# Keys put in order by blocks of 16 heads in an attention kernel, with three of the eight blocks and the second chunk's adjacency squares moved inside the first chunk

## The chip, the cores and the metric

The kernel runs on one NeuronCore of a Trainium2 chip. The metric is the device time of one execution in microseconds (us). A core has five engines that run their own instruction queues in order: PE (TensorE, matmuls), DVE (VectorE), ACT (ScalarE), POOL (GpSimd) and SP (SyncE, which here only issues DMA transfers). They wait for each other and for transfers through semaphores. Sixteen DMA engines carry the transfers.

## The reference

Four graph layers over 3327 nodes with 128 features and an adjacency matrix `adj` (3327 x 3327). Nearly all of the time is the first layer, an attention whose "heads" come from a plain reshape of the projections:

```python
def _L0_gnn_ref(x, spatial_encoding, edge_encoding, Wq, Wk, Wv, Wo):   # both encodings are adj
    n, d = x.shape                       # 3327, 128
    h = Wq.shape[0] // d                 # 8
    scale = d ** (-0.5)
    q = (x @ Wq.T).reshape(d, n, h)      # 128 heads, each n keys of 8 elements
    k = (x @ Wk.T).reshape(d, n, h)
    v = (x @ Wv.T).reshape(d, n, h)
    a = jnp.einsum('dnh,dmh->dnm', q, k) * scale
    a = a + spatial_encoding + edge_encoding
    a = jax.nn.softmax(a, axis=2)
    out = jnp.einsum('dnm,dmh->dnh', a, v)
    return out.reshape(n, h * d) @ Wo.T
# x = x + layer 0..3 of relu(layernorm(x)); layers 1 to 3 are dense products with adj
```

So there are 128 heads of head size 8, and each one adds the same matrix 2 adj to its 3327 x 3327 scores.

## The kernel before

**Prelude.** The nodes are normalised and projected, 13 steps of two node tiles each. The keys go to DRAM as they come out (`kraw_d`, one row of 128 heads x 3327 keys for each of the 8 elements e), the queries to `qS_d`. Then the values are projected in 13 more steps, and in the last eight of these `k_halves(e)` puts the keys of element e in order: it loads all 128 heads of that element (one head to a partition, 3327 keys), and for each of two halves r of the key tiles ACT rounds them to the matmul's 32-bit format (`hi`), DVE subtracts (`lo`), and SP stores both to `kS_d`, [2 halves, 8 elements, 128 heads, 3328 keys]. The tile framework orders this part by itself. A kernel branch then follows (`tc.If(loose < 1)`); the attention is inside it.

**Attention.** The queries are cut into 7 chunks c of 476 columns. In a chunk there are 32 groups g of 4 heads; in a group 13 units q, each a pair of key tiles (the even and the odd one, r = 0 and 1). This part is ordered by hand (`manual_schedule`): one loop over slots, four to a unit, writes out every engine's queue. In a unit DVE first puts adj minus a bound on the row's maximum into a PSUM bank (`seed`), PE adds the scores of the four heads one after the other (`scores`: each head's product comes with the previous head's taken away), ACT takes the exponential after each (`exps`), and PE multiplies with the values into `po` (`values`). In units 0, 2, 5, 7 and 10 of each group (`BY_HAND`), DVE works one exponential itself as a polynomial (`hand_exp`), so that these units and those behind them are fuller on DVE than units 4, 9 and 12.

**What a group needs from DRAM.** In unit 1 of a group, `loads` issues for the next group 16 key transfers (`KT<-kS_d`, `load_k`), the first queries (`load_q`) and the values (`VR`). In units 3, 5 and 7 POOL writes negated queries (`negate_q`) and SP issues the next head's queries. In unit 8 POOL spreads the values (`spread_v`) and touches the last keys (`all_here`, tile `seen`). The next group's first score matmul waits for `seen`. All these transfers are issued on SP's one queue, in the order in which the loop writes them. In the program's order of waits SP's transfers take turns on eight semaphores, and one waits for the one eight before it to have landed, so that at most eight are under way.

**The squares.** A chunk's seeds need adj transposed (`adjT`) and a bound for each query row (`bound_d`). Both are made for the next chunk during the present one, by squares of 128 rows, 4 or 3 to a chunk (22 in all inside chunks 0 to 5: four in chunk 0 and 18 after it). `plan(u, f)` hangs a step on unit u; it is written out at the unit's start, after the first step of `hand_exp`. For each of a square's four quarters j, in one group each, the steps are: `load` (4 transfers of adj rows into the tile `rows`), two `turn`s (DVE transposes 13 tiles each into the tile `cols`), `largest` (DVE, row maxima). After the fourth quarter come `gather` (4 transfers with 4 bytes a row to `rowmax_d`), `back` (one transfer that reads them again, tile `four`), `finish` (two small DVE operations that wait for `four`, then the transfer `bound_d<-b`) and `store` (one transfer of `cols` to `adjT`, 3328 packets of 512 bytes). Both tiles exist once. Before the change, with u the start of the group after the fourth quarter:

```python
sq, u = Square(e_t, s), (c * NG + 7 * k + 1) * NQ
for j in range(4):
    plan(u, sq.load, j)
    plan(u + 4, sq.turn, j, 0)
    plan(u + 9, sq.turn, j, 1)
    plan(u + 12, sq.largest, j)
    u += NQ
for k, f in ((0, sq.gather), (1, sq.back), (7, sq.finish), (8, sq.store)):
    plan(u + k, f)
```

After the attention come the dense products of layers 1 to 3, which the change does not touch.

Of the kernel before, what the change touches and what calls it, by code (L numbers as in the profile page):

```python
# [10 lines left out]
F32 = mybir.dt.float32  # L11
# [3 lines left out]
F32R = mybir.dt.float32r  # L15
I32 = mybir.dt.int32
AF = mybir.ActivationFunctionType
ALU = mybir.AluOpType
# [4 lines left out]
P = 128  # L23
N = 3327
D = 128
H = 8
HD = D * H
NT = 26
NP = NT * P
NQ = NT // 2  # L30

KW = NP // 4
HEADS = D
GN = HEADS * N
GP = GN + 4 * P
NC = 7
CW = 476
AW = 19 * NT
NG = HEADS // 4
HALF_SCALE = 0.5 * D ** -0.5  # L40


# [46 lines left out]
def gnn_kernel(ctx: ExitStack, tc: tile.TileContext, x, adj, Wq, Wk, Wv, Wo, embed, layer,  # L89
               embed_bias, layer_bias, weight, bias, W_in, W_out, out):  # L90
    nc = tc.nc
# [11 lines left out]
    kraw_d = dram.tile([H, GP], F32, name="kraw_d")  # L103

    qS_d = dram.tile([2, H, GP], F32, name="qS_d")
    kS_d = dram.tile([2, H, HEADS, NP], F32, name="kS_d")
# [36 lines left out]
    class Small:  # L143


        def __init__(self, pool, pre):
            self.pool, self.pre, self.n = pool, pre, 0
# [116 lines left out]
    class Square:  # L264
# [8 lines left out]
        def load(self, j):  # L273
            if j == 0:
                self.cols = self.pool.tile([P, NT, P], F32, name="cols")
            self.rows = self.pool.tile([P, KW], F32, name="rows")
            n0 = self.s * P + 32 * j
            m = min(32, N - n0)
            if m < 32:
                nc.gpsimd.memset(self.rows, 0.0)  # L280
            for i in range(4):
                w = KW - (i == 3)
                nc.sync.dma_start(self.rows[32 * i:32 * i + m, :w], adj[n0:n0 + m, i * KW:i * KW + w])
            nc.gpsimd.memset(self.rows[96:P, KW - 1:KW], NOTHING)
# [27 lines left out]
    def square(pool, s, small):  # L312
        q = Square(pool, s, small)
        for j in range(4):
            q.load(j)
            q.turn(j, 0)
            q.turn(j, 1)
            q.largest(j)
        q.store()
        return q  # L320

    def head_rows(tensor):

        return bass.AP(tensor=tensor.tensor, offset=tensor.offset, ap=[[N, HEADS], [1, N]])

    with tc.tile_pool(name="a1", bufs=1) as a1, tc.tile_pool(name="a2", bufs=2) as a2, \
# [6 lines left out]
        h = a1.tile([P, NT, D], F32, name="h")  # L333
# [16 lines left out]
        for t0 in range(0, NT, 2):  # L350
            for s in "kq":
# [3 lines left out]
                for i in range(2):  # L355
                    t = t0 + i
                    sq = a4.tile([P, H, P], F32, name="sq")
                    for b in range(2):
                        ps = projected(s, t, b)
                        by_e = ps.rearrange("p (e i) -> p e i", e=4)  # L360
                        part = (slice(None), slice(4 * b, 4 * b + 4), slice(i * P, (i + 1) * P))
# [11 lines left out]
                for half in range(2) if s == "q" else ():  # L373
                    nc.sync.dma_start(places(qS_d, t0, 2, H, half * H * GP), st[half].bitcast(F32))
                nc.gpsimd.dma_start(bass.AP(tensor=n2_d[s].tensor, offset=n2_d[s].offset + t0 * P,
                                            ap=[[NT * P, P], [1, 2 * P]]), n2.rearrange("p t i -> p (t i)"))
# [32 lines left out]
            nc.vector.tensor_scalar(wide, fm1, BOUND_MAX, None, op0=ALU.is_gt)  # L409
            return wide  # L410

        def k_halves(e):
            raw = a2.tile([P, NP], F32, name="st_q0")
            nc.gpsimd.memset(raw[:, N:NP], 0.0)
            nc.sync.dma_start(raw[:, :N], head_rows(kraw_d[e]))
            of = raw.rearrange("d (p q r) -> d r q p", q=NQ, r=2)
            for r in range(2):
                hi = a2.tile([P, NQ, P], F32R, name="st_k0")
                lo = a2.tile([P, NQ, P], F32R, name="st_q1")
                nc.scalar.copy(hi, of[:, r])  # L420
                nc.vector.tensor_tensor(lo, of[:, r], hi.bitcast(F32), op=ALU.subtract)
                for i, half in enumerate((hi, lo)):
                    nc.sync.dma_start(kS_d[i, e, :, r * NQ * P:(r + 1) * NQ * P],
                                      half.bitcast(F32).rearrange("d q p -> d (q p)"))

        v_rows = v_d.rearrange("(p t) d -> p t d", t=NT)
        for t0 in range(0, NT, 2):
            if t0 == 0:
                wide = bound_scores()
            if t0 >= 10:  # L430
                k_halves(t0 // 2 - 5)
            sv = a2.tile([P, 2, HD], F32, name="st_v")
            for i in range(2):
                for b in range(2):
                    evac(sv[:, i, b * 512:(b + 1) * 512], projected("v", t0 + i, b))
            nc.gpsimd.dma_start(v_rows[:, t0:t0 + 2], sv)
# [3 lines left out]
    with tc.tile_pool(name="d1", bufs=1) as d1, tc.tile_pool(name="d2", bufs=2) as d2, \  # L440
# [17 lines left out]
        with tc.If(loose > 0):  # L458
            for s in range(squares_of(0), NT):
                square(d2, s, d2)  # L460
            for t in range(NT):
                m = rows_of(t)
                ar = d1.tile([P, NP], F32, name="ar")
# [61 lines left out]
    with tc.tile_pool(name="e1", bufs=1) as e1, tc.tile_pool(name="e_adj", bufs=28) as e_adj, \  # L525
# [73 lines left out]
        with tc.If(loose < 1), tc.manual_schedule():  # L599
# [80 lines left out]
            def bare(c, q):  # L680

                w = width_of(c)
                nc.scalar.activation(EA[q][:, :w], EA[q][:, :w], AF.Exp, scale=2.0)
# [71 lines left out]
            def plan(u, f, *a):  # L755
                behind.setdefault(u, []).append((f, a))

            def plan_squares(c):
                for k, s in enumerate(range(squares_of(c), squares_of(c + 1))):
                    sq, u = Square(e_t, s), (c * NG + 7 * k + 1) * NQ  # L760
                    for j in range(4):
                        plan(u, sq.load, j)
                        plan(u + 4, sq.turn, j, 0)
                        plan(u + 9, sq.turn, j, 1)
                        plan(u + 12, sq.largest, j)
                        u += NQ
                    for k, f in ((0, sq.gather), (1, sq.back), (7, sq.finish), (8, sq.store)):
                        plan(u + k, f)

            for j in range(4):  # L770
# [18 lines left out]
                        plan(u - (7 if c else 1), bare, c, q)  # L789
            shifted(0, 0)  # L790
            bare(0, 0)

            def in_slot(i):

# [715 lines left out]
```

## Time and profile before

| what | value |
| --- | --- |
| time, median of 3 runs | 10971.67 us (10970.61 to 10973.61) |
| profiled execution, its own time | 10981.99 us |
| its span, first to last instruction | 10980.2 us, so 1.8 us lie around it |
| PE busy | 10536.5 us (96%) |
| ACT busy | 10031.9 us (91%) |
| DVE busy | 8481.1 us (77%) |
| POOL busy | 1532.1 us (14%) |
| prelude: first instruction behind the branch | 419.65 us |
| first score matmul | 456.16 us |
| first and last copy of `po` (one to a group, 224) | 511.6 and 10172.7 us |
| a `turn`, a `largest` on DVE (median) | 991 and 1011 ns |
| granted TensorE clock, mean | 0.984 |

The 224 copies of `po` are 223 groups apart, so a group takes 43.3 us on average and a unit 3.33 us. In the timelines a line reads: start in us, length in us, engine, line of kernel.py, operation, out<-in by the program's tile names, count; in brackets the time that the engine sat idle before it, and what ended that. SPq is SP issuing transfers: its length is that of the issuing, not of the transfer. The line numbers are those of the kernel before.

### The profile page before, as it was taken

What the parts mean: (1) busy time and instruction counts of PE and PEld (TensorE: products, weight loads), DVE (VectorE), ACT (ScalarE), POOL (GpSimd) and SP (SyncE); (2) the same over time, 40 slices, a digit from 0 to 9 for tenths busy, and PEclk for the clock granted to TensorE, in tenths of its full rate; (3) what the DMA queues carried; (4) which work ended last, traced back from release to release, by engine and by line L of the source; (5) the groups of instructions that cost most, each with busy time, mean ns of one, the idle gap of its engine ahead of it and who ended that gap; (6) DMA issues with size and microseconds to landing.
All of it is one profiled execution on the core that took longest, in us unless ns stands there. A gap on an engine that the chain in (4) does not pass through costs nothing. (4 is left out here: it accounts for less than half of the span.)

```text
span 10980.2 us, 204468 instructions
## 1 busy us (share of the span) xinstructions
PE 10536.5 (96%) x72876; PEld 3438.3 (31%) x72876; DVE 8481.1 (77%) x13503; ACT 10031.9 (91%) x13789; POOL 1532.1 (14%) x2480
## 2 busy tenths in 40 slices
PE   4599999999999999999999999999999999999889
PEld 2133333333333333333333323333323333333544
DVE  5588887888878887788887888878877777777655
ACT  3599999999999999999999999999999999999330
POOL 5011111111111111111111111111111111111101
PEclk7799999999999999999999999999999999999999
DMA  8865665665565565565556555565555555554678
GB/s 249 254 99 94 96 96 111 96 97 95 89 119 94 96 97 86 109 99 93 90 95 118 94 96 93 94 118 97 87 92 96 97 94 87 81 88 72 203 235 281
DMA packets 695338, 1256.97 MB, mean 114 GB/s; under 512 B 195218, under 2 KB 555049, under 8 KB 691244
## 3 DMA queue, kind: packets, MB, share of 16 engines
q1 hardware_dynamic: 644044, 1114.42, 55.4%
q0 software_dynamic: 50272, 129.37, 4.3%
q8 instruction: 586, 9.60, 0.4%
q14 instruction: 436, 3.57, 0.1%
HBM read 1096.53 MB, written 146.60 MB: 113 GB/s over the span
## 5 line engine op out<-in xcount | busy, mean ns | idle before, releaser
L666 ACT ACTIVATE e<-S 128x952 f32<-128x952 f32 (+1 forms) x9024 | 8366.0, 1102 | 40.3 <-PE S L654 33.6
L713 PE MATMUL po<-e,VA 128*9 128x476 f32 (+1 forms) x46592 | 5739.3, 565 | 33.1 <-DVE OS L721 12.6
L645 DVE TENSOR_TENSOR S<-a,shb 128x476 f32<-128x476 f32 (+1 forms) x5824 | 3940.7, 677 | 1450.4 <-ACT e L666 1062.5
L654 PE MATMUL S<-QS,KT 64*128 64x476 f32 (+1 forms) x22176 | 4533.8, 445 | 77.8 <-DMA a<-adjT 23.3
L654 PEld LDWEIGHTS S<-QS,KT 64*128 64x128 f32 x22176 | 2077.0, 184 | 5103.7 <-ACT e L666 1281.6
L669 ACT ACTIVATE e<-S 128x476 f32<-128x476 f32 (+1 forms) x4128 | 2476.1, 714 | 24.1 <-PE S L654 23.6
L695 DVE SCALAR_TENSOR_TENSOR e<-e,h 128x476 f32<-128x476 f32 (+1 forms) x2240 | 1493.9, 667 | 77.0
L713 PEld LDWEIGHTS po<-e,VA 128*9 128x9 f32 x46592 | 691.0, 88 | 1606.3 <-issue 1487.9
L570 POOL TENSOR_SCALAR QS<-QS 128x476 fp32r<-128x476 f32 (+1 forms) x669 | 484.8, 725 | 4292.9 <-DMA QS<-qS_d 2457.6
L725 POOL DMA_DIRECT2D oT_d<-OS x896 | 471.9, 532 | 3665.3 <-DVE OS L721 3622.1
L691 DVE TENSOR_SCALAR h<-S 128x476 f32<-128x476 f32 (+1 forms) x1120 | 728.0, 650 | 327.0 <-PE S L654 322.5
L697 DVE SCALAR_TENSOR_TENSOR e<-e,EA 128x476 f32<-128x476 f32 (+1 forms) x1120 | 754.0, 673 | 0.0
L695 DVE SCALAR_TENSOR_TENSOR e<-h 128x476 f32<-128x476 f32 (+1 forms) x1120 | 743.6, 664 | 0.0
L1110 PE MATMUL pu<-strip,y 128*128 128x512 f32 (+2 forms) x1456 | 600.2, 566 | 30.3 <-DVE y L971 14.8
L654 PE MATMUL S<-QZ,KT 64*128 64x476 f32 (+1 forms) x1120 | 494.4, 441 | 10.6 <-DVE S L645 9.3
L1110 PEld LDWEIGHTS pu<-strip,y 128*128 128x128 f32 (+1 forms) x1456 | 271.4, 191 | 304.5 <-issue 271.1
L580 POOL COPY VA<-VR 128x832 f32<-128x832 f32 x224 | 245.6, 1097 | 24.7 <-DMA VR<-v_d 24.7
L1114 DVE TENSOR_REDUCE deg<-strip 128x1 f32<-128x1536 f32 (+1 forms) x104 | 193.7, 1881 | 62.1 <-DMA strip<-adjT 43.5
L654 PEld LDWEIGHTS S<-QZ,KT 64*128 64x128 f32 x1120 | 205.4, 183 | 87.1 <-DVE S L645 47.7
L288 DVE STREAM_TRANSPOSE cols<-rows 128x416 f32<-128x416 f32 x208 | 204.5, 988 | 30.6 <-DMA rows<-in_adj_dram 23.4
L721 DVE COPY OS<-po 128x476 f32<-128x476 f32 (+1 forms) x224 | 146.2, 653 | 88.8 <-PE po L713 88.8
L1063 ACT COPY uT<-pu 128x512 f32<-128x512 f32 (+1 forms) x21 | 11.1, 553 | 222.3 <-PE pu L1110 222.3
(256 smaller groups left out, 1956.7 us busy)
## 6 DMA issues: line engine op xcount, KB each, us to landing
KT<-kS_d SPq DMA_DIRECT2D x1792, 208.0 KB
KT<-kS_d SPq DMA_DIRECT2D x1792, 104.0 KB
VR<-v_d SPq DMA_DIRECT2D x224, 416.0 KB
QS<-qS_d SPq DMA_DIRECT2D x3072, 14.9 KB
QS<-qS_d SPq DMA_DIRECT2D x1536, 29.8 KB
adjT<-cols SPq DMA_DIRECT2D x26, 1664.0 KB
a<-adjT SPq DMA_DIRECT2D x156, 238.0 KB
strip<-adjT POOLq DMA_DIRECT2D x39, 895.5 KB, 5.5
```

The lines of the kernel that those rows point to most:

```text
L570: nc.gpsimd.tensor_scalar(QS[b][:, j + 1, :w], QS[b][:, j, :w].bitcast(F32), -1.0, 0.0, op0=ALU.mult, op1=ALU.add)
L580: nc.gpsimd.tensor_copy(VA[(c * NG + g) % 2][:, :, :, 0:H], v.rearrange("p j (t e) -> p t j e", e=H))
L645: touch(u, [r], nc.vector.tensor_tensor(bank(u, r), adj_of[c][2 * q + r][:, :w], shift_of[c][:, :w], op=ALU.subtract))
L654: x = nc.tensor.matmul(bank(u, r), KT[b][64 * r:64 * r + 64, max(0, j - 1), q * P:(q + 1) * P], q_s[64 * r:64 * r + 64, :w], start=hand an ...
L666: touch(u, (0, 1), nc.scalar.activation(e[:, :, :w], S[:, odd:even + 1, :w], AF.Exp, scale=2.0))
L669: touch(u, [r], nc.scalar.activation(e[:, 1 - r, :w], bank(u, r), AF.Exp, scale=2.0))
L691: touch(u, [1], nc.vector.tensor_scalar(s, bank(u, 1), EXP_ARG, None, op0=ALU.mult))
L695: nc.vector.scalar_tensor_tensor(e, s if k == 3 else e, EXP_C[k], s, op0=ALU.add, op1=ALU.mult)
L697: nc.vector.scalar_tensor_tensor(e, e, EXP_C[0], EA[pairs[u][2]][:, :w], op0=ALU.add, op1=ALU.mult)
L713: nc.tensor.matmul(po[32 * j:32 * j + H + 1, :w], VA[k % 2][:, 2 * pairs[v][2] + of, j, :], e_of[v, j][:, 1 - of, :w], start=(q == 0 and r ...
L725: nc.gpsimd.dma_start(oT_d[:, d * N + c * CW:d * N + c * CW + w], o[32 * j:32 * j + H + 1, :w])
L1110: nc.tensor.matmul(ps[:, :k], y[:m, t, :], s[:m, c * 4 * P - c0:c * 4 * P - c0 + k], start=(t == 0), stop=(t == NT - 1))
```

## The change

The keys are put in order by blocks b of 16 heads x 8 elements (128 partitions) instead of by element. Five blocks (`EARLY`) are done in the prelude, in its value steps 0, 2, 4, 6 and 8, as before on ACT and DVE (`k_block`). The other three (heads 80 to 127) are done inside chunk 0, planned from groups 16, 20 and 24 on (`Keys`): a load of 128 rows of 3327 keys into the tile `cols`, then four parts of 7 or 6 key tiles each; for each part DVE copies the rounded keys into the tile `rows` (`high`), SP stores them, POOL subtracts in place (`low`), SP stores again. The tile `rows` grows from 832 to 896 columns.

The squares of chunk 0 start at groups 0, 4, 8 and 12 instead of 1, 8, 15 and 22, one unit later within the group (unit 1), each next one right behind the last. Their `gather` and `store` come right before the next start. In all chunks `back` moves from 1 to 9 and `finish` from 7 to 12 units behind the group's start; in chunks 1 to 5 `gather` stays at 0 and `store` at 8.

In the order of the changed program's SP queue, chunks 1 to 5 have: `rowmax_d<-rm` x4, the 16 keys, values and queries of the next group, `adjT<-cols`, `four<-rowmax_d`, `bound_d<-b`, the next 16 keys. Before it was `rowmax_d<-rm` x4, `four<-rowmax_d`, the 16 keys, values and queries up to the third head's, `bound_d<-b`, the fourth head's queries, `adjT<-cols`, the next 16 keys.

```diff
--- before.py
+++ after.py
@@ -37,6 +37,8 @@
 CW = 476
 AW = 19 * NT
 NG = HEADS // 4
+KB = P // H
+EARLY = 5
 HALF_SCALE = 0.5 * D ** -0.5
 
 
@@ -273,7 +275,7 @@
         def load(self, j):
             if j == 0:
                 self.cols = self.pool.tile([P, NT, P], F32, name="cols")
-            self.rows = self.pool.tile([P, KW], F32, name="rows")
+            self.rows = self.pool.tile([P, 7 * P], F32, name="rows")[:, :KW]
             n0 = self.s * P + 32 * j
             m = min(32, N - n0)
             if m < 32:
@@ -318,6 +320,29 @@
             q.largest(j)
         q.store()
         return q
+
+    def k_rows(b):
+
+        return bass.AP(tensor=kraw_d.tensor, offset=kraw_d.offset + KB * b * N, ap=[[N, KB], [GP, H], [1, N]])
+
+    def k_store(b, i, r, q0, half):
+        m = half.shape[-1]
+        nc.sync.dma_start(bass.AP(
+            tensor=kS_d.tensor, offset=kS_d.offset + (i * H * HEADS + KB * b) * NP + (r * NQ + q0) * P,
+            ap=[[NP, KB], [HEADS * NP, H], [1, m]]), half)
+
+    def k_block(b, pool):
+        raw = pool.tile([P, NP], F32, name="st_q0")
+        nc.gpsimd.memset(raw[:, N:NP], 0.0)
+        nc.sync.dma_start(raw[:, :N], k_rows(b))
+        of = raw.rearrange("d (p q r) -> d r q p", q=NQ, r=2)
+        for r in range(2):
+            hi = pool.tile([P, NQ, P], F32R, name="st_k0")
+            lo = pool.tile([P, NQ, P], F32R, name="st_q1")
+            nc.scalar.copy(hi, of[:, r])
+            nc.vector.tensor_tensor(lo, of[:, r], hi.bitcast(F32), op=ALU.subtract)
+            for i, half in enumerate((hi, lo)):
+                k_store(b, i, r, 0, half.bitcast(F32).rearrange("d q p -> d (q p)"))
 
     def head_rows(tensor):
 
@@ -409,26 +434,12 @@
             nc.vector.tensor_scalar(wide, fm1, BOUND_MAX, None, op0=ALU.is_gt)
             return wide
 
-        def k_halves(e):
-            raw = a2.tile([P, NP], F32, name="st_q0")
-            nc.gpsimd.memset(raw[:, N:NP], 0.0)
-            nc.sync.dma_start(raw[:, :N], head_rows(kraw_d[e]))
-            of = raw.rearrange("d (p q r) -> d r q p", q=NQ, r=2)
-            for r in range(2):
-                hi = a2.tile([P, NQ, P], F32R, name="st_k0")
-                lo = a2.tile([P, NQ, P], F32R, name="st_q1")
-                nc.scalar.copy(hi, of[:, r])
-                nc.vector.tensor_tensor(lo, of[:, r], hi.bitcast(F32), op=ALU.subtract)
-                for i, half in enumerate((hi, lo)):
-                    nc.sync.dma_start(kS_d[i, e, :, r * NQ * P:(r + 1) * NQ * P],
-                                      half.bitcast(F32).rearrange("d q p -> d (q p)"))
-
         v_rows = v_d.rearrange("(p t) d -> p t d", t=NT)
         for t0 in range(0, NT, 2):
             if t0 == 0:
                 wide = bound_scores()
-            if t0 >= 10:
-                k_halves(t0 // 2 - 5)
+            if t0 % 4 == 0 and t0 // 4 < EARLY:
+                k_block(t0 // 4, a2)
             sv = a2.tile([P, 2, HD], F32, name="st_v")
             for i in range(2):
                 for b in range(2):
@@ -458,6 +469,8 @@
         with tc.If(loose > 0):
             for s in range(squares_of(0), NT):
                 square(d2, s, d2)
+            for b in range(EARLY, HEADS // KB):
+                k_block(b, d1)
             for t in range(NT):
                 m = rows_of(t)
                 ar = d1.tile([P, NP], F32, name="ar")
@@ -755,16 +768,46 @@
             def plan(u, f, *a):
                 behind.setdefault(u, []).append((f, a))
 
+            class Keys:
+
+                def __init__(self, b):
+                    self.b = b
+
+                def load(self):
+                    raw = e_t.tile([P, NT, P], F32, name="cols").rearrange("p t n -> p (t n)")
+                    nc.gpsimd.memset(raw[:, N:NP], 0.0)
+                    nc.sync.dma_start(raw[:, :N], k_rows(self.b))
+                    self.of = raw.rearrange("d (p q r) -> d r q p", q=NQ, r=2)
+
+                def high(self, r, q0, q1):
+                    self.part = e_t.tile([P, 7 * P], F32, name="rows")[:, :(q1 - q0) * P]
+                    nc.vector.tensor_copy(self.part.rearrange("d (q p) -> d q p", p=P).bitcast(F32R),
+                                          self.of[:, r, q0:q1, :])
+                    k_store(self.b, 0, r, q0, self.part)
+
+                def low(self, r, q0, q1):
+                    part = self.part.rearrange("d (q p) -> d q p", p=P)
+                    nc.gpsimd.tensor_tensor(part.bitcast(F32R), self.of[:, r, q0:q1, :], part, op=ALU.subtract)
+                    k_store(self.b, 1, r, q0, self.part)
+
+            def plan_keys():
+                for b in range(EARLY, HEADS // KB):
+                    u, keys = 4 * (b - 1) * NQ + 1, Keys(b)
+                    plan(u, keys.load)
+                    for hi, lo, r, h in ((7, 9, 0, 0), (13, 16, 0, 1), (22, 24, 1, 0), (26, 30, 1, 1)):
+                        plan(u + hi, keys.high, r, 7 * h, 7 + 6 * h)
+                        plan(u + lo, keys.low, r, 7 * h, 7 + 6 * h)
+
             def plan_squares(c):
                 for k, s in enumerate(range(squares_of(c), squares_of(c + 1))):
-                    sq, u = Square(e_t, s), (c * NG + 7 * k + 1) * NQ
+                    sq, u = Square(e_t, s), (c * NG + 7 * k + 1 if c else 4 * k) * NQ + (not c)
                     for j in range(4):
                         plan(u, sq.load, j)
                         plan(u + 4, sq.turn, j, 0)
                         plan(u + 9, sq.turn, j, 1)
                         plan(u + 12, sq.largest, j)
                         u += NQ
-                    for k, f in ((0, sq.gather), (1, sq.back), (7, sq.finish), (8, sq.store)):
+                    for k, f in ((0 if c else -1, sq.gather), (8 if c else -1, sq.store), (9, sq.back), (12, sq.finish)):
                         plan(u + k, f)
 
             for j in range(4):
@@ -789,6 +832,8 @@
                         plan(u - (7 if c else 1), bare, c, q)
             shifted(0, 0)
             bare(0, 0)
+
+            plan_keys()
 
             def in_slot(i):
 
```

## The prediction, made before the changed kernel ran

> **What bounds the kernel now.** I read the page's busy shares, a table by windows, the prelude's timeline, then SP's queue and DVE around one square, and last the longest stall of DVE inside the attention.
>
> ```profile
> PE 10536.5 (96%) x72876; PEld 3438.3 (31%) x72876; DVE 8481.1 (77%) x13503; ACT 10031.9 (91%) x13789; POOL 1532.1 (14%) x2480
> ```
>
> ```profile
> 350.00:400.00 50.00, 0.00 (x0) 0.00 (x0) 19.58 (x8) 22.73 (x9) 0.83 (x4) 0.51 0.92 368
> ...
> 600.00:700.00 100.00, 99.13 (x728) 30.07 (x728) 82.95 (x129) 99.93 (x139) 12.35 (x22) 1.00 0.58 87
> ```
>
> Columns after the window and its length: busy us and instructions of PE, weight loads, DVE, ACT, POOL; clock; DMA share; GB/s. The prelude's end (first row) is DMA alone: share 0.92, PE idle. In the attention PE and ACT are full, and 728 matmuls in 100 us is the pace with and without a square under way. So time is won only in the prelude, and in the attention lost only where PE is made to wait; nothing lost there is caught up.
>
> The prelude, the last pairs of elements:
>
> ```profile
> 358.36 1.37 SPq L415 DMA_DIRECT2D st_q<-kraw_d  x2
> 366.39 6.58 ACT L420 CAST st_k<-st_q 128x1664 fp32r<-128x1664 f32 x2 [11.81 <-DMA st_q<-kraw_d]
> ...
> 376.39 0.33 SPq L423 DMA_DIRECT2D kS_d<-st_q  x1
> ...
> 413.88 0.33 SPq L423 DMA_DIRECT2D kS_d<-st_q  x1
> 419.65 1.69 POOL L601 MEMSET VA<- 128x936 f32 x2 [34.11 <-SPq L458]
> ```
>
> SP's queue at the end of chunk 1's first square:
>
> ```profile
> 2059.24 1.75 SPq L299 DMA_DIRECT2D rowmax_d<-rm  x4
> 2066.97 0.38 SPq L304 DMA_DIRECT2D four<-rowmax_d  x1
> 2067.44 12.98 SPq L551 DMA_DIRECT2D KT<-kS_d  x16
> ...
> 2101.65 0.53 SPq L295 DMA_DIRECT2D adjT<-cols  x1
> 2105.18 12.61 SPq L551 DMA_DIRECT2D KT<-kS_d  x14
> ```
>
> The 4-byte writes of `gather` take about 6 us to land, `back` waits for that, and the keys start 6.3 us late (one group earlier they started at 2018.0, so 2061.1 was due). The store comes a whole group later. Its packets, two DMA views:
>
> ```profile
> DMA packets 3539, 2.16 MB, mean 196 GB/s; under 512 B 113, under 2 KB 3485, under 8 KB 3538
> ```
>
> ```profile
> DMA packets 150, 0.65 MB, mean 161 GB/s; under 512 B 53, under 2 KB 53, under 8 KB 150
> ```
>
> The first is 2101 to 2112, the second 2112 to 2116: the store's 3328 packets of 512 B are all in the first, so it takes up to 10.4 us. The store of 5183.91, which had no small write just before it, had all of them through by 5191.2: with the landing about 8 us. DVE at unit 12 of the same group:
>
> ```profile
> 2101.26 0.64 DVE L697 SCALAR_TENSOR_TENSOR e<-e,EA 128x476 f32<-128x476 f32 x1
> 2102.87 0.66 DVE L645 TENSOR_TENSOR S<-a,shb 128x476 f32<-128x476 f32 x1 [0.96 <-ACT e L666]
> ```
>
> The last rows show what a late DVE costs (here for a late `rows` in chunk 5), on DVE and on PE:
>
> ```profile
> 8187.75 0.65 DVE L697 SCALAR_TENSOR_TENSOR e<-e,EA 128x476 f32<-128x476 f32 x1
> 8197.31 0.96 DVE L288 STREAM_TRANSPOSE cols<-rows 128x416 f32<-128x416 f32 x1 [8.92 <-DMA rows<-in_adj_dram]
> ```
>
> ```profile
> 8191.77 0.69 PE L654 MATMUL S<-QS,KT 64*128 64x476 f32 x3
> 8200.33 0.76 PE L654 MATMUL S<-QZ,KT 64*128 64x476 f32 x1 [7.87 <-DVE S L645]
> ```
>
> A DVE wait of 8.9 us in a free unit cost PE 7.9: about 1 us is free.
>
> **1. Prelude.** In the changed program's order the first four blocks stand where the first four elements stood, with the same loads, casts and stores; then one block comes in place of four elements. It is the first of the pair loaded at 358.36: its fourth store is the one of 376.39. From the last store to the first instruction behind the branch it was 419.65 - 413.88 = 5.8 us, so that instruction comes at 382.2: **-37**. Bounds -30 (the four stores, now 16 x 8 rows in eight places, each take 2 us more) and -42 (no second load in the same queue).
>
> **2. `back` leaves the keys' way (18 squares, chunks 1 to 5).** Mostly hidden before: `seen` lay 9 us ahead of the first scores in a group without squares (1701.5 against 1712.2). Groups with it lost little, one 6 us (copies of `po` at 5145.2 and 5194.5, 49.3 apart instead of 43.1). Together **-10** (0 to -13).
>
> **3. `finish` behind the store (the same 18).** The change lets `store` pass ahead of `back` in SP's queue, and `finish` waits for `four` at unit 12 of that very group, on DVE, with the next seeds behind it. From the free time of the key buffer, t = 2061.1: an undisturbed group has its last queries issued 34.7 us after the first keys (1711.34 to 1746.0). The first four key pieces now go at t, the rest when the 4-byte writes have landed at about t+5, 2 us late: last queries t+37, store t+37.3, landed t+45.6 (8.3 us), `four` right behind it in the same queue, t+46.2. DVE reaches `finish` when the polynomial ends, 2101.9 = t+40.8. It waits 5.4 us; the two small operations add 0.4, and 0.96 was idle: 4.9 for PE, say 5. 18 x 5 = **+90**. Bounds: 3 each with the queries at t+35 (+54); 8.5 with them at t+38.5 and a 10.4 us store (+153).
>
> The Trainium skill (page "DMA: Bandwidth & Descriptors", section "Specifications") gives about 358 GB/s as a core's HBM limit; by that the store's 1.70 MB would land in an estimated 4.8 us, each wait would shrink to about 1.5 us and this term to about 27 us. The 8.3 to 10.4 us of the trace decide. The same page ("Queues, rings and completion order") says that descriptors are taken in ring order and a completion signal lands only after earlier writes of its DMA engine; that speaks against putting a waited-for read behind a long store.
>
> **4. Chunk 0, more steps on the same queues.** No row shows these together; bounds by the nearest.
> - Three square-to-square joints: `gather`, `store` and the next four loads now go ahead of the keys. The 16 keys take 20.5 us to land once started; they start when the store has landed, some 12 us late, against the 9 us of cover of `seen`. 3 each, **+10** (0 to 20).
> - `finish` of these squares at the next unit 0: `back` is issued after the late queries: 3 us of DVE wait each, three times, **+9** (0 to 15).
> - The joint to block 5: its load goes into `cols`, so SP waits for the store to land and then the load takes 4 to 8 us; keys 17 late less 9, +8; and that square's `four` stands behind the first `high` and `low` stores, +9: **+17** (5 to 30).
> - The three blocks: the second and fourth `high` are planned in unit 1, the store of the `low` before in SP's queue behind the fourth head's queries, 7 us before the next keys. `high` store 3 us (a store of twice the size took 3.4), POOL 1.8 us by its 512-column sum (996 ns), 3.5 if strides double it, `low` store 3 us: DVE waits 1 to 3 us for `rows` twice a block, and the keys behind it start 7 late, inside the cover. Each `high` is 896 x 2.0 ns = 1.8 us (by the prelude's strided subtraction, 3333 ns for 1664), or 0.6 by a contiguous pass (1954 ns for 3328); 0.8 stand out in full units. 2 x 2.5 + 1 + 4 x 0.8 = 9, three times **+27** (6 to 45).
> - Turns and `largest`, one unit later, fall in units 5, 10 and 0, which are DVE's own. There DVE idles 0.4 to 0.6 us before a seed and the step takes 1.0: 0.3 x 48 = **+14** (0 to 24).
>
> The sum is +77 (30 to 130). The three blocks' 15 MB find DMA at a share of 0.58 here, and POOL is 14% busy: both are cover; without it the keys would be late in every group. The wider `rows` and the untaken branch cost nothing.
>
> **Sum.** -37 - 10 + 90 + 77 = +120 on the profiled execution's 10981.99, so 11102. The median of the runs lies 10.3 us lower: 11092.
>
> **Rivals.** (A) *Faster: the read of `rowmax_d` passes the store.* If `four` lands within 3.5 us of its issue, unit 12 waits for nothing and term 3 is zero; with chunk 0 at 20, -37 - 10 + 20 = -27: 10945. For it: sixteen DMA engines and a tiny read. Against: the keys of 2105.18 do not show their packets until the store's are done. (B) *The store takes 10.4 us each time*, because the queue is as busy as at 2101: term 3 is 18 x 8 = 144, 11146. (C) *The prelude's gain does not come*: eight places for each store and load make one block as slow as two elements, the branch is left at about 413 and the gain is 6: 11123.
>
> **Chances.** Forecast 0.53, A 0.15, B 0.14, C 0.10, and 0.08 that the gain and a small term 3 cancel. A measurement of this kernel can tell about 0.2% (22 us) from no change; A lies 27 below, and one case in seven of it falls inside that bound: faster 0.13, same 0.10, slower 0.77. The range, 10950 to 11205, begins just above A, takes in the low ends of terms 3 and 4 (-42 - 13 + 54 + 30 = +29, so 11001) and the cancelling case, and goes up to their high ends not quite all together; half of A and the extreme of B are left out.
>
> **What would show it.** Right: the first instruction behind the branch near 382; in chunks 1 to 5, 18 DVE waits of 4 to 8 us before the reduction of `four`, put down to its transfer, and PE gaps of the same size; those groups 48 us apart by the copies of `po`, all others 43.1; chunk 0 some 75 us above 32 x 43.1. Wrong: no DVE wait at `four` (A), waits near 10 (B), the branch left at 410 or later (C), or chunk 0 as smooth as before.

## The result, and the profile after

The changed kernel takes 11095.5 us (median; 11090.1 to 11113.6) against 10971.1 us before, a ratio of 1.0116 (95% interval 1.0098 to 1.0133): about 124 us slower. The forecast was 11092. That it came so close is partly luck: one step of the sum failed by 27 us and another was too large by some 40, in opposite directions. Besides, the forecast went from a profiled execution that lay 10 us above its median, and the one profiled here lies 5 us below its own: between the two profiles the time grows by 108 us, where the sum has +120.

The page's busy shares after:

```profile
PE 10586.5 (95%) x72876; PEld 3444.5 (31%) x72876; DVE 8484.0 (77%) x13509; ACT 10024.4 (90%) x13783; POOL 1561.8 (14%) x2492
```

The instructions of PE are the same in number; the span has grown by 108 us, 10980.2 to 11088.3, and PE is busy for 50 us more of it. The table by windows, with the columns of before:

```profile
350.00:400.00 50.00, 9.44 (x17) 3.33 (x15) 14.36 (x10) 13.04 (x9) 1.60 (x3) 0.67 0.80 250
600.00:700.00 100.00, 94.64 (x680) 28.65 (x672) 78.54 (x123) 93.83 (x128) 12.05 (x20) 0.97 0.65 102
```

The first row is the prelude's end: DMA moves 250 GB/s here where it moved 368, and PE still has V work (17 matmuls) that had been done by 350 us before. The second row is in chunk 0: 680 matmuls instead of 728, so PE waits.

The end of the prelude in the timeline, the last block from its load to the first instruction behind the branch:

```profile
373.42 2.59 SPq L337 DMA_DIRECT2D st_q<-kraw_d  x1
...
392.60 6.58 ACT L342 CAST st_k<-st_q 128x1664 fp32r<-128x1664 f32 x2 [19.29 <-DMA st_q<-kraw_d]
402.54 0.54 SPq L330 DMA_DIRECT2D kS_d<-st_q  x1
410.66 1.69 POOL L614 MEMSET VA<- 128x936 f32 x2 [35.62 <-SPq L469]
```

One load takes 19 us where a load at the same place took 8 (358.36 to 366.4). Not all of that is the load's own doing: in the trace's packet records the stores of V (8192 bytes a packet) go on until about 389 here and were through by 359 before, and this load's packets took 0.55 us (median) against 0.50 for an element's. The branch is left at 410.7, only 9 us earlier than at 419.65.

One square of chunk 1, its second: SP's queue, then DVE and PE around unit 12.

```profile
2468.92 0.56 SPq L297 DMA_DIRECT2D adjT<-cols  x1
2469.53 4.12 SPq L306 DMA_DIRECT2D four<-rowmax_d  x1
2478.53 0.36 SPq L312 DMA_DIRECT2D bound_d<-b  x1
```

```profile
2472.77 0.65 DVE L710 SCALAR_TENSOR_TENSOR e<-e,EA 128x476 f32<-128x476 f32 x1
2478.15 0.16 DVE L310 TENSOR_REDUCE b<-four 128x1 f32<-128x4 f32 x1 [4.73 <-DMA four<-rowmax_d]
```

```profile
2477.06 0.69 PE L667 MATMUL S<-QS,KT 64*128 64x476 f32 x3
2480.59 0.75 PE L667 MATMUL S<-QZ,KT 64*128 64x476 f32 x1 [2.84 <-DVE S L658]
```

The read of `four` is issued right behind the store and comes back 8.6 us later; DVE stands for 4.7 us; the seed behind it is late, and PE stands for 2.8. The whole group is 4.6 us longer than 43.1, because the matmuls behind the wait are slow as well: the granted clock (third number from the end) is at half just then.

```profile
2480.60:2484.00 3.40, 3.40 (x13) 0.89 (x13) 3.19 (x5) 1.15 (x2) 0.00 (x0) 0.51 0.60 24
```

All squares together, from the view of the tile `four` (idle us of DVE, times):

```profile
  DMA four<-rowmax_d: 75.7, 21
```

Before, this line did not exist.

Chunk 0, where the last square hands over to block 5: SP's queue and PE.

```profile
1177.11 0.56 SPq L779 DMA_DIRECT2D cols<-kraw_d  x1
1177.78 20.56 SPq L564 DMA_DIRECT2D KT<-kS_d  x16
...
1216.62 1.53 PE L667 MATMUL S<-QS,KT 64*128 64x476 f32 x4 [9.47 <-POOL seen L597]
```

SP waits for the adj store to land (1177.1), loads the block, and the keys behind it need 20.6 us to be issued (12.3 to 13 in groups without a square). PE stands for 9.5 us, and another 6.7 at 1229.1 behind this square's late `four`. The group is 66.7 us long by the copies of `po`.

By those copies the span's 108 us divide so: prelude to the first copy -10.4; chunk 0 +78.1 (1420.2 us for 31 groups, 1342.1 before); chunks 1 to 5 +39.5; chunk 6 and all behind it +0.9. Chunk 0 by itself, from its first copy to its last, before and after:

```profile
511.55:1853.65 1342.10, 1329.69 (x9674) 407.58 (x9676) 1088.14 (x1673) 1338.71 (x1823) 180.53 (x294) 1.00 0.60 99
501.20:1921.40 1420.20, 1355.95 (x9674) 410.54 (x9676) 1112.87 (x1683) 1346.57 (x1823) 209.72 (x308) 0.98 0.62 104
```

The same 9674 matmuls keep PE busy 26.3 us longer, at a mean clock of 0.98 instead of 1.00; the other 51.8 of the 78.1 us are idle time of PE. In chunks 1 to 5 the 39.5 us are 24.3 of idle time and 15.2 of slower matmuls. In the attention of the changed kernel the granted clock falls to half 19 times, for 3.4 to 10.2 us (3 times before), and each time this begins during a gap of PE of 1.3 us or more, or within 2 us after one. So a wait of PE costs more than its own length here.

### The profile page after: what moved, and what is told of

The parts are those of the page before. It is cut to its first block, busy times and chain, and to the rows that moved or that the text cites. A ratio compares the mean times of both kernels' runs of the same rounds, so it can differ in the third digit from the quotient of the medians.

```text
span 11088.3 us, 204505 instructions
## 1 busy us (share of the span) xinstructions
PE 10586.5 (95%) x72876; PEld 3444.5 (31%) x72876; DVE 8484.0 (77%) x13509; ACT 10024.4 (90%) x13783; POOL 1561.8 (14%) x2492
## 5 line engine op out<-in xcount | busy, mean ns | idle before, releaser
L658 DVE TENSOR_TENSOR S<-a,shb 128x476 f32<-128x476 f32 (+1 forms) x5824 | 3945.6, 677 | 1432.5 <-ACT e L679 1040.3
```

Source lines behind the costliest of these rows:

```text
L658: touch(u, [r], nc.vector.tensor_tensor(bank(u, r), adj_of[c][2 * q + r][:, :w], shift_of[c][:, :w], op=ALU.subtract))
```

## Experiments

Landing times below are issues and completions as the trace has them. "Square groups" are groups 5, 12, 19 and 26 of chunks 1 to 5: their sum above 43.1 us each was 13.7 before and is 54.4 after. Each time stands beside the runs of the kernel before on the same chip, whose median was 10969 to 10981.

**The finish alone.** `e1_finish_later`:

```diff
-  ... (9, sq.back), (12, sq.finish)):
+  ... (9, sq.back), (17 if c else 12, sq.finish)):
```

> The changed kernel with one number changed: in chunks 1 to 5 the step that reduces the four bounds (finish) runs five units later, at unit 17 instead of 12, that is in unit 4 of the next group. Theory (finish waits on DVE for a read that stands behind the adj store in SP's queue, and PE pays): the 18 DVE waits of 2 to 5 us before the reduction go, the groups 5, 12, 19 and 26 of chunks 1 to 5, 54 us above 43.1 in the changed kernel, fall to within 5 us in sum, and the time falls by about 50, from 11095 to some 11045. Rival (the groups are long because the late store and its read hold up the next keys, not DVE): the DVE waits go but the groups stay long, time within 15 us of 11095.

Measured 11052.9 us, 43 below the changed kernel (1.0066 of before, 1.0049 to 1.0083). The line for the tile `four` now reads:

```profile
  DMA four<-rowmax_d: 12.2, 4
```

These four are chunk 0's. The square groups stand 3.4 us above 43.1 in sum. So the wait on DVE is the whole of it: 54.4 - 3.4 = 51 us in the profile. Chunks 1 to 5 together are 47 us shorter than in the changed kernel: 30 us less idle time of PE, and 18 less for the same 49922 matmuls (6871.95 us busy instead of 6889.56).

**The same move in the kernel before.** `e2_before_late_back`:

```diff
-  ((0, sq.gather), (1, sq.back), (7, sq.finish), (8, sq.store)):
+  ((0, sq.gather), (8, sq.store), (9, sq.back), (12, sq.finish)):
```

> The kernel before with the offsets of the changed one alone: store at unit 8, back at unit 9, finish at unit 12, for all squares of the attention; prelude and placing of the squares as before. Theory (this move costs about 54 in waits and gives about 14 back, independent of the rest): some 40 us slower than before in chunks 1 to 5 and some 5 to 15 more for the four squares in chunk 0, so 11010 to 11030. Rival (the waits come from the squares being crowded or shifted by the new chunk 0): within 15 us of 10971.

Measured 11059.3 us, +81 (1.0074; 1.0057 to 1.0091), more than expected. DVE waited for `four` 22 times, 89.7 us in all; square groups 68.9, chunk 0 14 us longer. The cost belongs to the order of these steps, not to the new chunk 0.

**The good order by itself.** `e6_before_good_order`, the kernel before:

```diff
+  ((0, sq.gather), (8, sq.store), (9, sq.back), (17, sq.finish)):
```

> The kernel before with the squares' steps in a third order: store at unit 8, back at unit 9, finish at unit 17 (unit 4 of the next group). Theory (the changed kernel's early store and late back are good by themselves and only its finish is too early): the late keys of before go without a new wait, the groups 5, 12, 19 and 26 of chunks 1 to 5 stand within 5 us of 43.1 in sum (13.7 before, 68.9 with finish at unit 12), time 5 to 15 us below the kernel before. Rival (the queue pays somewhere else for the store ahead of the read): same as before or slower.

Measured 10978.8 against 10980.4 (0.9997; 0.9987 to 1.0007): no difference that can be told; the 5 to 15 us that were expected are not seen. The profile does show the late keys gone (square groups 3.3 instead of 13.7), so the 10 us of step 2 exist in this view, but the times can't confirm them.

**Eight blocks in the elements' places.** `e4_blocks_in_place`, the kernel before with the changed kernel's `k_block`:

```diff
-                k_halves(t0 // 2 - 5)
+                k_block(t0 // 2 - 5, a2)
```

> The kernel before with only the shape of the eight key steps in the prelude changed: eight blocks of 16 heads x 8 elements at the places where the eight elements of 128 heads stood, all in the prelude, nothing moved to the attention. The bytes and the number of transfers are the same. Theory (a block is slower than an element by its addresses): with 150 us for five blocks against 154 for eight elements, a block costs up to 1.5 times an element, and the prelude becomes 30 to 80 us longer, time 11000 to 11050; chunks 0 to 6 as before within 5 us. Rival (blocks cost what elements cost, and the gain was lost because the V work of the prelude is late): within 10 us of 10971.

Measured 11013.2, +35 (1.0032; 1.0020 to 1.0045). The branch is left at 456.5, 36.8 later than with elements, and nothing else moved (chunk 0 at 1341.4). The same bytes in the same number of transfers cost 4.6 us more for each block. The mark in the timeline is how soon ACT gets the buffer of a first store back. First the kernel before, then this one:

```profile
369.73 0.34 SPq L423 DMA_DIRECT2D kS_d<-st_k  x1
373.21 3.39 ACT L420 CAST st_k<-st_q 128x1664 fp32r<-128x1664 f32 x1 [0.24 <-DMA kS_d<-st_k]
```

```profile
430.87 0.58 SPq L329 DMA_DIRECT2D kS_d<-st_k  x1
436.33 3.34 ACT L341 CAST st_k<-st_q 128x1664 fp32r<-128x1664 f32 x1 [2.19 <-DMA kS_d<-st_k]
```

3.5 us against 5.5. SP too needs 0.58 us instead of 0.34 to issue it. The changed kernel has five such blocks: taking three out gives 456.5 - 410.7 = 46 us, and the shape had taken 37 of them beforehand.

**Why a block is slow.** Four kernels ask whether it is the addresses. `e3_element_major`, the changed kernel:

```diff
-  ap=[[N, KB], [GP, H], [1, N]])
+  ap=[[GP, H], [N, KB], [1, N]])
   ...
-  ap=[[NP, KB], [HEADS * NP, H], [1, m]]), half)
+  ap=[[HEADS * NP, H], [NP, KB], [1, m]]), half)
```

> The changed kernel with the 128 rows of a block taken in another order: partition = element x 16 + head instead of head x 8 + element, in load and store alike; the same bytes and packets. Theory (a block's transfers are slow because neighbouring partitions lie in eight far places): a store alone lands in 3.4 to 4 us instead of 5.4, a load alone in 8 to 10, the prelude's end comes 20 to 30 us earlier (first instructions behind the branch at 382 to 392 instead of 411), time 11065 to 11075. Rival (eight far places cost as much in any order, or something else than the transfers is late): prelude's end within 5 us of 411, time within 10 us of 11095.

Measured 11201.0 (1.0206; 1.0189 to 1.0223); branch left at 465.4, a lone store (one with little else under way) 8.5 to 10 us. Both expectations failed: it is much worse. The trace shows nine completions for each of these transfers where the others have sixteen. For the store issued at 442.72 the first of the nine comes 1.1 us after the issue and the other eight 6.8 to 8.5 us after it (of the sixteen of an element's store none comes before 3.2 us): with a first dimension of 8, eight engines carry it. So this run does not tell about addresses. The Trainium skill (page "DMA: Bandwidth & Descriptors", section "Rules for kernel authors") says that an outermost dimension of size c below 16 confines a transfer to at most c engines; the eight late completions fit that.

`e5_spread_heads`, as e4:

```diff
-  kraw_d.offset + KB * b * N, ap=[[N, KB], [GP, H], [1, N]])
+  kraw_d.offset + b * N, ap=[[H * N, KB], [GP, H], [1, N]])
```

and the store alike.

> Eight blocks in the prelude at the elements' places, as in e4, but each block takes every eighth head (b, b + 8, ...) instead of 16 neighbours. The number, size and bytes of the transfers stay; the sixteen first-dimension steps of a transfer now lie 104 KB apart, as they do for an element, instead of 13 KB. Theory (near addresses taken at the same time are what makes a block slow): a store alone lands in 3.4 to 4 us instead of 5.4, the first instruction behind the branch comes near 420 instead of 456.5, time within 12 us of the kernel before (10978). Rival (the far steps from element to element within one row group are what is slow): stores stay at 5.4, the branch is left between 450 and 460, time 11005 to 11020.

Measured 11019.5 (1.0035; 1.0023 to 1.0047), branch left at 462.0, a lone store 5.4 us. Near addresses are not the cause.

`e9_rows_together`, the changed kernel:

```diff
-  kS_d = dram.tile([2, H, HEADS, NP], F32, name="kS_d")
+  kS_d = dram.tile([HEADS, 2, H, NP], F32, name="kS_d")
   ...
-  ap=[[NP, KB], [HEADS * NP, H], [1, m]]), half)
+  ap=[[2 * H * NP, KB], [NP, H], [1, m]]), half)
```

> The changed kernel with another layout of kS_d: head, half, element, position instead of half, element, head, position. In a block's stores the eight rows of one head now lie side by side (they were 1.7 MB apart); its load still reads eight far rows. The loads of KT read the same rows, now side by side too. Theory (far steps from row to row are what makes a block's transfer slow): a store alone lands in 3.4 to 4 us instead of 5.4, the load of a block alone stays slow, the branch is left 8 to 20 us earlier than 410.7, time 11070 to 11090, or less where the KT loads gain too. Rival (far steps are not it; the packets of a transfer whose rows are given by two dimensions are slow anyway): stores stay above 5 us, the branch is left within 5 us of 410.7.

Measured 11114.1 (1.0131; 1.0114 to 1.0148); a lone store 5.4 us, branch left at 406.7. So far steps are not the cause either. The square groups rose to 83 us. The store of adj is no slower here (7.8 us on average, 7.9 in the changed kernel), but the last queries ahead of it are issued 36.4 us after the first keys instead of 35.5, and DVE's waits for `four` in the 18 squares sum to 79 us instead of 64; what delays the queries stays open.

`e12_one_dimension`, e5 with the rows in another order, so that one pitch describes a store:

```diff
-  ap=[[H * NP, KB], [HEADS * NP, H], [1, m]]), half)
+  ap=[[H * NP, P], [1, m]]), half)
```

> e5 (eight blocks in the prelude, every eighth head, the places of the elements) with the 128 rows in the order element x 16 + head. In this order the rows of a store lie at one pitch of 104 KB, so the store is written with one dimension of 128 rows instead of 16 by 8; its bytes, packets and addresses are the same as in e5. The load has no such pitch and goes by 8 by 16 rows, as in e3, where the trace has nine completions for it instead of sixteen. Theory (a transfer is at full pace when one dimension of 128 rows is dealt to the engines as it is for an element, wherever the rows lie; two dimensions, or 80 rows, are dealt in a way that makes the engines share something): a lone store lands in 3.4 to 3.6 us as for an element, against 5.4 in e5 and 8.5 in e3, while the loads stay as slow as in e3 (20 us or more), so the prelude ends late all the same, at 440 to 500 and the time is 10990 to 11060. Rival (far rows themselves are slow): stores at 5 us or more.

Measured 11041.9 (1.0054; 1.0037 to 1.0070). The store issued at 475.20 landed in 3.4 us, that of 428.25 too: the pace of an element, at the very addresses of e5. Issuing one costs SP 0.33 us again, and from the last store to the first instruction behind the branch it is 5.6 us (479.22 to 484.84), 5.8 in the kernel before and 7.0 in e4.

So what makes a block's store slow is that its 128 rows are written as 16 by 8; one dimension of 128 rows took 3.4 us for both sets of addresses. From e5 to e12 the order of the rows in the partitions changed too, but that is not it: three different orders written as 16 by 8 (e4, e5, e9) all took 5.4 us. The loads, 8 by 16 here, took 18.5 to 38 us and the prelude ended late all the same. In the trace's packet records a 13,308-byte packet of a load takes 0.50 us for an element and 0.94 for a block of e4. The Trainium skill (page "DMA: Bandwidth & Descriptors", section "The descriptor swizzle") states that a 128-partition transfer is dealt so that each engine serves the partitions of one SBUF port. If 16 by 8 rows are dealt by eights instead, two engines would meet at one port, which would fit packets twice as long; no run here shows which engine carried which row.

**Mending chunk 0.** `e7_gaps`, the changed kernel with finish at unit 17 and:

```diff
-  u = (c * NG + 7 * k + 1 if c else 4 * k) * NQ + (not c)
+  u = (c * NG + (7 if c else 8) * k + 1) * NQ
   ...
-  u, keys = 4 * (b - 1) * NQ + 1, Keys(b)
+  u, keys = (8 * (b - EARLY) + 6) * NQ, Keys(b)
   ...
-  ((7, 9, 0, 0), (13, 16, 0, 1), (22, 24, 1, 0), (26, 30, 1, 1)):
+  ((9, 12, 0, 0), (17, 20, 0, 1), (25, 28, 1, 0), (35, 37, 1, 1)):
```

> The changed kernel with finish at unit 17 and another plan for chunk 0: its four squares every eight groups from group 1, at the units that the other chunks use, and one block of keys in each gap between two squares, its load after the next group's keys in SP's queue, its four roundings in units 9, 4, 12 and 9. The same work in all. Theory (of the 78 us in chunk 0, 23 are the joint between square and block, 14 the steps in hand units, 14 the joints between squares, and 27 the blocks' waits and roundings): only 5 to 8 us a block stay, chunk 0 takes 1355 to 1370 for 31 groups instead of 1420, time 10985 to 11005. Rival (the blocks' bytes and POOL work are the cost, wherever they stand): chunk 0 at 1390 or more, time above 11020.

Measured 11015.6 (1.0032; 1.0021 to 1.0044). Chunk 0 takes 1390.5 us, at the rival's edge: the squares now cost nothing, but the three blocks cost 19, 14 and 17 us in their groups, two to three times what I allowed.

`e10_keys_by_pool`, e7 with:

```diff
-  nc.sync.dma_start(raw[:, :N], k_rows(self.b))
+  nc.gpsimd.dma_start(raw[:, :N], k_rows(self.b))
   ...
-  nc.vector.tensor_copy(self.part...
+  nc.gpsimd.tensor_copy(self.part...
```

stores by `nc.gpsimd` too, units 9, 11, 13, 15, 22, 24, 26, 28.

> e7 with all of a block's steps in chunk 0 on POOL: its load and stores from POOL's queue instead of SP's, its four roundings by POOL instead of DVE, in units 9, 0, 9 and 0. The same bytes. Theory (a block costs 16 us in e7 because its stores stand in SP's queue waiting for POOL's or DVE's work, so the next keys and queries come late, and because DVE waits): the keys' loads of the groups with a block start within 3 us of 43.1 after those before, chunk 0 takes 1350 to 1365 for 31 groups (1390.5 in e7), time 10975 to 10992. Rival (the bytes that a block moves while keys and queries load are the cost, or POOL becomes late for the queries' signs): chunk 0 at 1380 or more.

Measured 11010.2 (1.0037; 1.0023 to 1.0052), chunk 0 at 1391.4: taking SP and DVE out of a block's steps gained nothing. The reason stands in the timelines of POOL and of DVE at one subtraction:

```profile
780.88 2.26 POOL L790 TENSOR_TENSOR rows<-cols,rows 128x768 fp32r<-128x768 f32 x1 [2.78 <-DMA kS_d<-rows]
```

```profile
781.45 3.74 DVE L658 TENSOR_TENSOR S<-a,shb 128x476 f32<-128x476 f32 x3
```

Three seeds are 2.0 us of work and take 3.7: the one begun beside POOL's subtraction ends 0.5 us after it. The seeds (L658) of a group without and of one with a block; behind the window and its length stand DVE's busy us and count, clock, DMA share and GB/s:

```profile
621.30:664.40 43.10, 17.39 (x27) 1.00 0.58 92
765.90:814.10 48.20, 22.40 (x26) 1.00 0.57 109
```

5.0 us more for one seed less, in a group that is 5.1 longer. In all of e10, 22 DVE instructions with two inputs from SBUF (seeds and steps of the polynomial) took 34.0 us longer than usual, and each of them ended 0.51 to 0.53 us after a POOL instruction on a block. In e7 it is 12 instructions and 24.7 us, beside 18.0 us of DVE's own roundings, so that moving the roundings to POOL mostly exchanged the one for the other.

The kernel before shows the same on a small scale. There 132 seeds begin during the POOL copy `VA<-VR` (`spread_v`, 1.1 us); all of them end 0.50 to 0.65 us after it and take 0.97 us on average, against 0.66 for a seed that meets no POOL instruction. The 26 instructions `h<-S`, whose one input lies in PSUM, that begin during such a copy take 0.65 us as always.

PE's waits in chunk 0 of e10 (us in total, times, longest):

```profile
PE S L667 <- DVE S L658: 25.6, 29, 3.1
PE S L667 <- POOL seen L597: 7.0, 3, 3.2
```

Before, the first was 1.7 and the second nothing. With 19.9 us of slower matmuls (1349.56 us busy instead of 1329.69) this makes up the 49 us that chunk 0 is longer, so the waits for seeds are the larger part; whether POOL or the block's bytes make `seen` late is open. The Trainium skill (page "SBUF — State Buffer", section "Who interferes with whom") says that a VectorE instruction with two SBUF inputs contends with a GpSimd instruction that reads SBUF, through a read interface that they share, and calls the shared ports an exclusive lock. These rows agree.

`e11_both`, e10 with the layout of e9:

> e10 and the layout of kS_d of e9 together. Each theory adds: what e9 gains against the changed kernel and what e10 gains against e7 come together, 10960 to 10985. Rival (one of them changes nothing): as the other alone.

Measured 11018.7 (1.0043; 1.0026 to 1.0060): nothing gained over e10, as the rival said.

**Fewer bytes in the old shape.** `e8_elements_80`, e7 with the prelude's blocks replaced by element steps on the first 80 heads:

```diff
-  if t0 % 4 == 0 and t0 // 4 < EARLY:
-      k_block(t0 // 4, a2)
+  if t0 >= 10:
+      k_halves(t0 // 2 - 5)
```

> e7 with the prelude's five blocks taken as eight element steps of 80 heads each, at the places where the kernel before has its eight steps of 128 heads: five eighths of the bytes in the shape of before, 16 times as many transfers of less size than in e7's prelude per byte moved. Theory (a block's shape ate the prelude's gain): the element steps move 15 MB less at the pace of before, so the first instruction behind the branch comes at 380 to 392 instead of 411, and the time is 20 to 30 us below e7, some 15 us or more below the kernel before. Rival (the prelude is held by the number of steps or by ACT and DVE, whose instructions are as long on 80 partitions as on 128): branch left at 405 or later, time within 10 us of e7.

(It is 40 transfers instead of 25 in the prelude, 1.6 times as many, not 16.) Measured 11030.1 (1.0042; 1.0026 to 1.0059), 14 us above e7, and the branch is left at 430.9, 11 us later than with 128 rows and 17 later than with e7's blocks. A lone store of 80 rows took 3.55 us, no less than one of 128; a packet of a load took 0.95 us instead of 0.50; and ACT's and DVE's passes are as long on 80 partitions (6.58 us for two, as before). One pair of elements takes 32.1 us (363.04 to 395.12) instead of 27.5. My theory that bytes set the prelude's length fell here; the rival had the late branch right, but not a time within 10 us of e7.

No version beat the kernel before; e6 can't be told from it.

## Why the prediction was right, and where it was not

**What bounds the kernel**: held as far as it went. The attention lost time only where PE waited, for DVE's seeds (page: matmuls of QS waited 115 us instead of 78, those of QZ 47 instead of 11) and for the loads. But idle time is not all of it: of the 117.6 us that chunks 0 to 5 grew by, 76 are gaps of PE and 41 the slower matmuls behind them, for which the sum had no term. The prediction's own last rows show it. After the gap of 7.87 us the clock is at 0.50 from 8194.5 to 8204.7, and the group is 53.1 us long by the copies, 10.0 above 43.1: a DVE wait of 8.9 us cost 10.0, and nothing was free.

**Step 1, the prelude, failed.** I took -37 (-30 to -42) because a block stands in an element's place "with the same loads, casts and stores". It came to -9 at the branch. The shape costs 4.6 us a block (e4), through transfers whose rows are given as 16 by 8 (e12). Rival C had the right event (gain 6) and the right cause in words, eight places for each store and load, but gave it 0.10; the places were not the reason, the two dimensions were. My upper end of 2 us for each of four stores looked only at the last store and not at the load: the first load of a pair landed in 8 to 9 us before and in 14 to 16 in e4's last two pairs. By e4's price five blocks would have left the branch at 382 + 23 = 405. The other 5 us fit the 19 us of the last load, beside which V's stores were still under way; no run tests that by itself.

**Step 2, -10**: seen in the profile (13.7 to 3.4 in e1), too small for the times of e6.

**Step 3, the finish behind the store: right mechanism, too large.** Eighteen squares, each with the store ahead of the read in one queue; DVE waited in 17 of them. Forecast +90 (54 to 153), measured 51 (e1). Two inputs were too high: the last queries came 35.5 us after the first keys on average, not 37, and the store landed mostly in 7.6 us (8.4 to 9.0 in four), not 8.3. DVE waited 3.6 us on average instead of 5.4, and a square cost 2.8 us instead of 5, of which some 1.6 are a gap of PE and 1.0 slower matmuls. The 51 us are one profile's figure: with the same order of steps the square groups stood 69 us above 43.1 in e2, 67 in e3 and 83 in e9, against 3 with the late finish, so that other builds fall inside the forecast's bounds, still below its middle. Rivals A (the read passes) and B (10.4 us each) are out: the read came back with the store each time, and the store took 9.0 us at most.

**Step 4, chunk 0: +78 measured, +77 forecast, with its parts shifted.** By the group lengths: three joints and finishes 14 (19 forecast); the joint to block 5 24 (17); the three blocks 32 (27); the other groups of the first half, with steps in hand units, 9 (14). The blocks' price was right for a partly wrong reason: I counted POOL as cover, and its subtraction holds DVE's seeds (14.8 us of DVE time in the changed kernel), and 26 of the 78 us are slower matmuls, which no part of the sum had. That the total fits is luck. Two smaller slips: the cover of `seen` is 10.7 us by the two times given for it, not 9, and the ends of the parts add up to 11 and 134, not 30 and 130.

**Sum.** -10 + 39 + 78 + 1 = +108 against a forecast +120. The prelude gave 27 us less than forecast, chunks 1 to 5 cost 41 less (+39 instead of +80).

## What to carry to other kernels

Before a small read is moved behind a large store in one queue, ask when its consumer runs: the order store, read, finish was free as soon as finish stood five units later. When a transfer is re-cut, compare not bytes and packets but how its rows are described; a shape that the trace has never shown is a term with a wide range, in loads as in stores. Price a wait of PE by how much longer its group became, not by the gap alone. An engine that is 14% busy is no cover if its instructions hold up those of a fuller one.

## What the runs showed of the hardware

- The same 0.83 MB to the same addresses landed in 3.4 us as one dimension of 128 rows (e12) and in 5.4 us as 16 by 8 (e5); a store of that size with a first dimension of 8 (e3) took 8.5 to 10, on eight engines.
- A store of 80 rows took as long as one of 128 (3.55 us against 3.4), and packets of a load of 80 rows nearly twice as long (0.95 us against 0.50).
- A DVE seed of 0.67 us begun beside a POOL subtraction of 2.3 us took 2.2 us and ended 0.5 us after it (e10). So did all 132 seeds begun during a POOL copy in the kernel before: they ended 0.50 to 0.65 us after it.
- A 2 KB read issued 0.6 us behind a 1.7 MB store in the same queue came back with the store, 7.2 to 8.6 us after its issue, in every square of chunks 1 to 5.
- Behind gaps of PE the granted clock fell to half for 3.4 to 10.2 us: chunk 0's 9674 matmuls kept PE busy for 1355.95 us at a mean of 0.98, and for 1329.69 us at 1.00 in the kernel before.
